# A four-layer network on one core: the front of layer 1 in two parts, and the group norm's small products tied to the scan's order

## The chip, the cores and the metric

The kernel runs on one core of one Trainium2 chip. Five engines work side by side, each through its own queue in order: TensorE (PE; its weight loads are shown as PEld), VectorE (DVE), ScalarE (ACT), GpSimd (POOL), and SyncE (SP), which here only issues DMAs. The metric is the device time in microseconds of one execution, as a median of several runs. A profile is one more execution, recorded by the hardware; its engines' busy times and waits come from that one.

## What is computed

The input is 16 images of 192 channels and 32 x 32 pixels, in fp32. Four layers follow one another, each as `x = x + layer(group_norm(x))`:

```python
x = x + L0(_gn(x))   # mLSTM block, a linear branch, 3x3 convolution, batch norm, leaky ReLU
x = x + L1(_gn(x))   # layer norm, a Mamba block, layer norm, projection
x = x + L2(_gn(x))   # depthwise 3x3 convolution, batch norm, clip to 0..6
x = x + L3(_gn(x))   # four Mamba scans of the image, depthwise branch, router
```

The group norm has 32 groups of 6 channels; each group of an image is brought to mean 0 and variance 1:

```python
def _gn(v, G=32, eps=1e-5):
    g = v.reshape(B_, G, C_ // G, H_, W_)
    m = jnp.mean(g, axis=(2, 3, 4), keepdims=True)
    s = jnp.var(g, axis=(2, 3, 4), keepdims=True)
    return ((g - m) / jnp.sqrt(s + eps)).reshape(v.shape)
```

The core of layer 1 is the Mamba recurrence over 1024 tokens, for 384 channels and 16 states n:

```python
dA = jnp.exp(dt_t[..., None] * A[None])
h = dA * h + (dt_t * x_t)[..., None] * B_t[:, None, :]
y = jnp.einsum('bdn,bn->bd', h, C_t)
```

Layer 3 has the same recurrence four times an image, in four directions.

## The kernel before

The program runs layer 0, then layers 1 and 2 together, then layer 3. A batch norm over all images separates them (layer 0 ends in one, layer 2 in one), so nothing of a later part can begin before the earlier part's last image is done.

Layers 1 and 2 (`layer12`, L1071) are one long scan of 32 units, two halves of 512 tokens for each of the 16 images. A unit has 16 steps, one for each state n, so an image has 32 steps and the part 512. One step (`scan_run`, L942) is: ACT makes three decays `da` (L987) and three scaled inputs `xbt` (L967); PE turns the inputs over into the PSUM tile `xb` (L995, L998); DVE runs three recurrences of 128 x 512 (L1011) into `h`; POOL multiplies `h` by C (L1018), which SP has loaded as `cb` two steps ahead (L969); PE adds the result into `y` (L1029), two steps later. All the scan's PE instructions are tied into one order by hand: the inner function `in_order` makes each depend on the one before, without a semaphore.

Everything else of layers 1 and 2 is side work, written as generators and handed out between the scan's instructions by the class `Side` (L210). `side.add(kind, steps, start, end)` gives a window in scan steps. At each `tick(now)` a task goes on while the units that it has yielded stay below its share of the window:

```python
share = self.totals.get(kind, self.total) * (now - start) / (end - start)
while now >= end or (task[4] < share and now >= task[5]):
```

`totals` is what the kind came to the last time (24 before that). A yielded number counts as so many units; a yielded `Wait(n)` forbids the task to go on before n steps have passed; at the end of the window all that is left is handed out at once. What is handed out is placed by a scheduler that knows the data's dependences; the engines then take their queues in order.

In an image's 32 steps the windows are, before: prep of the second half (steps 1 to 13), gating of the image before (2 to 3.5), its output product (`layer1_out`, 3.5 to 8), the gate branch of this image (`layer1_gate`, 8 to 12.5), the front of the next image (`layer1_front`, 12.5 to 20), the tail of the image before (`layer1_tail`, 13.5 to 25), gating of this image's first half (18 to 21), the convolution of the next image (`layer1_conv`, 20 to 26), layer 2 of the image before (25.5 to 34), and prep of the next image's first half (26 to 30).

`layer1_front` (L1223) loads the input x and layer 0's result, applies layer 0's batch norm and leaky ReLU in four pieces (ACT L1234, DVE L1235), adds x in four pieces (DVE L1236), stores the sum, takes the group norm, normalises (L1241), stores the result, and then goes straight on to the layer norm and the first half of the input projection (L1254 to L1259), whose result goes through DRAM to the convolution. Its tile `x1` first holds the sum and then the layer norm's result, which `layer1_gate` reads until step 12.5. `layer1_out` and `layer1_tail` share another tile of the same size, `xt`; both tiles have one buffer.

`group_norm` (L344) serves all layers. Four `bn_stats` and two `bn_aggr` on DVE give each channel's mean and variance; a product with a 96 x 96 matrix (PE, L355) averages the means over the six channels of a group; DVE copies the result out of PSUM (L357), takes the channel's difference from it (L359), squares it (L361) and adds the variance (L362); a second product (L365) averages that; ACT makes the inverse root (L367, L368). The two products have two columns each. They take a bank of the PSUM pool `mm`, which has two, for all of the side work.

Layer 0 has its own chain of PE instructions (`Chain`, L244, kept as `self.main`) and its own windows, and layer 3 calls `scan_run` with 128 units, 2048 steps.

Of the kernel before, what the change touches and what calls it, by code (L numbers as in the profile page):

```python
# [243 lines left out]
class Chain:  # L244
# [5 lines left out]
    def __call__(self, ins):  # L250
        if self.last is not None:
            why = mybir.DependencyInfo(mybir.DependencyClass.NoSync, mybir.DependencyReason.DATA)
            self.tc.add_manual_dep(ins.ins, self.last, why)
        self.last = ins.ins.name
        return ins
# [19 lines left out]
class Program:  # L275
# [68 lines left out]
    def group_norm(self, pool, psum, x):  # L344
# [4 lines left out]
        for m in range(2):  # L349
# [3 lines left out]
            yield 1  # L353
        ps = psum.tile([128, 512], F32, name="mm")
        nc.tensor.matmul(ps[:HP, :2], self.k("group", HP), mv[:, :, 0], start=True, stop=True)  # L355
        mean = pool.tile([HP, 2], F32, name="gnmean")
        nc.vector.tensor_copy(mean, ps[:HP, :2])  # L357
        d = pool.tile([HP, 2], F32, name="gnd")
        nc.vector.tensor_tensor(d, mv[:, :, 0], mean, SUB)  # L359
        q = pool.tile([HP, 2], F32, name="gnq")  # L360
        nc.vector.tensor_tensor(q, d, d, MUL)  # L361
        nc.vector.tensor_tensor(q, q, mv[:, :, 1], ADD)  # L362
        yield 1
        ps = psum.tile([128, 512], F32, name="mm")
        nc.tensor.matmul(ps[:HP, :2], self.k("group", HP), q, start=True, stop=True)  # L365
# [27 lines left out]
    def layer0(self):  # L393
        tc = self.tc
        with (
# [13 lines left out]
            self.main = Chain(tc)  # L409
            for b in range(1, self.nb):  # L410
# [19 lines left out]
            side.close()  # L430
            finish(self.layer0_spread(self.nb - 1, wp, dp))
# [510 lines left out]
    def scan_run(self, units, side, bp, psum):  # L942
# [7 lines left out]
        last = []  # L950

        def in_order(ins):

            if last:
                self.tc.add_manual_dep(
                    ins.ins, last.pop(), mybir.DependencyInfo(mybir.DependencyClass.NoSync, mybir.DependencyReason.DATA)
                )
            last.append(ins.ins.name)
# [97 lines left out]
        for i in range(len(steps) - 2, len(steps)):  # L1056
            for t in range(3):
                total(i, t)
        side.close()
# [11 lines left out]
    def layer12(self):  # L1071
        tc = self.tc
        with (
# [7 lines left out]
            self.rep = 18 * (W + 2), 6  # L1081
            self.stats = wp.tile([HP, 2, 2 * self.nb, 6], F32, name="stats")
# [18 lines left out]
            for b in range(self.nb):  # L1101
                at = 2 * NS * b
                side.add("prep", prep(units[2 * b + 1]), at + 1, at + 13)
# [3 lines left out]
                side.add("silu", self.layer1_gate(b, bp, psum), at + 8, at + 12.5)  # L1107
                if b + 1 < self.nb:
                    side.add("front", self.layer1_front(b + 1, sp, bp, psum), at + 12.5, at + 20)
                if b:  # L1110
                    side.add("tail", self.layer1_tail(b - 1, sp, bp, dp, psum), at + 13.5, at + 25)
# [600 lines left out]
```

## Time and profile before

| | us |
|---|---|
| median of three runs | 17126.98 |
| the three runs | 17106.91 to 17131.63 |
| the profiled execution's own time | 17158.12 |
| its span, first to last instruction | 17156.3 |
| first scan of layers 1 and 2 starts at | 3755.3 |
| first scan of layer 3 starts at | 7540.7 |
| last scan of layer 3 starts at | 17089.1 |

The profiled execution took 31 us longer than the median. The busy time of an engine is the union of its instructions' times; the waits of an engine are its idle stretches, each put down to the instruction that ended it. The granted clock of TensorE is 0.959 on average. Of the DMA engines 29.7% of the time is used, and the core moves 90 GB/s.

The costliest rows of the page are the scan's own: POOL's product L1018 (2560 times, 3469 ns each, 8871.5 us), ACT's decays L987 (7680 times, 714 ns), DVE's recurrence L1011 (7680 times, 1202 and 1263 ns), and PE's transposes L1029, L995 and products L998. The side work's rows are much smaller: the first small product of the group norm, L355, is two passes of 0.22 us in each of the 64 norms; the additions L1236 take 1.37 us each in the steady part, the normalisation L1241 1.80 us.

### The profile page before, as it was taken

Reading aid. Unit: us, or ns where it says so; the run is one execution under the profiler, and the core shown is the slowest. Engines: PE = TensorE matmul, PEld = TensorE weight load, DVE = VectorE, ACT = ScalarE, POOL = GpSimd, SP = SyncE. Lnnn points to the kernel's source line nnn. Section 1 sums busy time; section 2 is a strip of 40 time slices with the busy share of each in tenths; the row PEclk is TensorE's granted clock in tenths of the full one; section 3 lists DMA queues with packets and bytes.
Section 4 is the critical chain, followed back from the end, with each engine's and each line's share of the span. In section 5 each row is a group of like instructions: output and inputs, shape, how many; then the busy total and the mean of one; then the engine's idle time right before and its main releaser. Section 6 shows DMA issues by size and latency. Waiting matters only on the chain. (4 is left out here: it accounts for less than half of the span.)

```text
span 17156.3 us, 262939 instructions
## 1 busy us (share of the span) xinstructions
PE 15613.4 (91%) x99452; PEld 10979.0 (64%) x99452; DVE 13102.8 (76%) x14795; ACT 11895.7 (69%) x19766; POOL 11422.4 (67%) x5491
## 2 busy tenths in 40 slices
PE   7999999979999999979999999999999999999998
PEld 4444444446555555647777777777777777777777
DVE  4555455547777777758888888988888898888888
ACT  3333333337666766748888888888888888888888
POOL 3334443436555555638888888878888888888888
PEclk8999999989999999989999999999999999999999
DMA  1111111123334443333333323333332333333232
GB/s 52 45 47 45 47 45 46 42 76 108 117 119 121 120 120 115 100 101 107 93 96 101 109 83 101 109 91 97 100 108 84 101 109 92 96 100 107 86 98 67
DMA packets 890140, 1544.64 MB, mean 90 GB/s; under 512 B 83472, under 2 KB 314653, under 8 KB 879530
## 3 DMA queue, kind: packets, MB, share of 16 engines
q1 hardware_dynamic: 888874, 1527.81, 29.7%
q8 instruction: 788, 12.91, 0.3%
q14 instruction: 478, 3.92, 0.1%
HBM read 1284.22 MB, written 243.27 MB: 89 GB/s over the span
## 5 line engine op out<-in xcount | busy, mean ns | idle before, releaser
L1018 POOL TENSOR_TENSOR h<-h,cb 128x1536 f32<-128x1536 f32 x2560 | 8871.5, 3469 | 1439.4 <-DVE h L1011 961.0
L987 ACT ACTIVATE da<-dt,neg_a 128x512 f32<-128x512 f32 x7680 | 5267.1, 714 | 1618.4 <-DVE h L1011 1565.5
L1011 DVE TENSOR_TENSOR_SCAN h<-da,carry,xb 128x512 f32<-128x512 f32 x3840 | 4653.2, 1263 | 708.8 <-PE xb L998 672.9
L1029 PE MATMUL y<-const,h 128*128 128x128 f32 x30720 | 4710.0, 276 | 127.4 <-DVE ysum L1469 54.0
L1011 DVE TENSOR_TENSOR_SCAN h<-da,xb 128x512 f32<-128x512 f32 x3840 | 4440.8, 1202 | 388.3 <-PE xb L998 272.1
L995 PE MATMUL xb<-const,xbt 128*128 128x128 f32 x23040 | 4057.7, 281 | 379.4 <-DVE h L1011 219.9
L967 ACT ACTIVATE xbt<-ut,bt 128x384 f32<-128x384 f32 x7680 | 4174.4, 603 | 210.3 <-PE xb L995 208.7
L1029 PEld LDWEIGHTS y<-const,h 128*128 128x128 f32 x30720 | 3677.9, 143 | 343.6 <-issue 288.4
L995 PEld LDWEIGHTS xb<-const,xbt 128*128 128x128 f32 x23040 | 2750.2, 142 | 1744.0 <-issue 616.2
L998 PE MATMUL xb<-diag,ut 128*128 128x128 f32 x15360 | 3015.1, 278 | 0.0
L998 PEld LDWEIGHTS xb<-diag,ut 128*128 128x128 f32 x15360 | 2382.8, 195 | 97.9 <-issue 97.9
L831 POOL TENSOR_TENSOR hs<-h,mhm 128x384 f32<-128x384 f32 x128 | 108.5, 848 | 1570.7 <-DVE den L836 735.6
L977 POOL TENSOR_TENSOR diag<-const,bt 128x512 f32<-128x512 f32 x640 | 687.0, 1074 | 575.3 <-PE xb L998 320.8
L1017 POOL COPY carry<-h 128x3 f32<-128x3 f32 x1280 | 249.1, 195 | 1222.7 <-DVE h L1011 978.2
L705 POOL TENSOR_TENSOR e<-e,const 128x1536 f32<-128x1536 f32 x128 | 443.3, 3464 | 244.0 <-DMA e<-row 226.9
L520 PE MATMUL conv<-ya,w_conv 128*64 128x512 f32 (+1 forms) x1152 | 500.9, 646 | 99.4 <-DMA ya<-yrows 61.2
L917 PE MATMUL mm<-dbl,w_dt 45*128 45x512 f32 x960 | 536.1, 642 | 33.4 <-DVE v L1491 16.1
L711 ACT ACTIVATE e<-e 128x1536 f32<-128x1536 f32 x128 | 189.7, 1482 | 445.6 <-POOL e L706 445.6
L780 PEld LDWEIGHTS num<-v,p 128*128 128x128 f32 x3072 | 386.6, 200 | 123.6 <-issue 50.8
L921 DVE SCALAR_TENSOR_TENSOR dt<-lnsq,mm 128x512 f32<-128x512 f32 x480 | 322.2, 671 | 184.1 <-ACT lnsq L920 184.1
L1172 PE MATMUL mm<-rep,taps 128*32 128x512 f32 x3072 | 423.8, 607 | 27.9 <-DMA rep<-xr 17.8
L1172 PE MATMUL mm<-rep,t_dw 96*32 96x512 f32 x2304 | 427.0, 618 | 22.1 <-DMA rep<-xr 15.9
(273 smaller groups left out, 17446.6 us busy)
## 6 DMA issues: line engine op xcount, KB each, us to landing
cb<-row SPq DMA_DIRECT2D x2560, 256.0 KB
rep<-xr SPq DMA_DIRECT2D x384, 331.0 KB
e<-row SPq DMA_DIRECT2D x128, 768.0 KB
rep<-xin SPq DMA_DIRECT2D x384, 256.0 KB
rep<-xr SPq DMA_DIRECT2D x384, 228.8 KB
x<-x SPq DMA_DIRECT2D x48, 768.0 KB
xr<-xin SPq DMA_DIRECT2D x48, 612.5 KB
xr<-xpad SPq DMA_DIRECT2D x32, 867.0 KB
```

What stands on the lines that cost most here:

```text
L520: nc.tensor.matmul(o, self.w_c2[:k, t, c0 : c0 + o.shape[0]], src[:k, r0 : r0 + 16, dx : dx + W], start=t == 0, stop=t == 14, skip_group_c ...
L705: nc.gpsimd.tensor_tensor(k.e, k.e, self.k0("mask")[:, None, :].to_broadcast([128, NH, 128]), ADD)
L917: nc.tensor.matmul(ps, w_dt[:, t * 128 : (t + 1) * 128], dbl, start=True, stop=True)
L967: nc.scalar.activation(t[:, c], u.ut[:, c], AF.Copy, scale=u.bt[:, c, n : n + 1])
L977: nc.gpsimd.tensor_tensor(d, ident[:, None, :].to_broadcast([128, 4, 128]), u.bt[:, 3, n : n + 4][:, :, None].to_broadcast([128, 4, 128]), ...
L987: nc.scalar.activation(da[i, t], u.dt[:, t], AF.Exp, scale=u.neg_a(t, n))
L995: in_order(nc.tensor.transpose(xb[i, t][:, c * 128 : (c + 1) * 128], xbt[i][:, c, t * 128 : (t + 1) * 128], ident))
L998: in_order(nc.tensor.matmul(xb[i, t][:, 384:], u.ut[:, 3, t * 128 : (t + 1) * 128], u.diag[n // 4][:, n % 4], start=True, stop=True, skip_ ...
L1011: nc.vector.tensor_tensor_scan(hv, dv, xv, 0.0 if first else u.carry_in[:, n, t : t + 1], MUL, ADD)
L1018: nc.gpsimd.tensor_tensor(h[i], h[i], u.c.pop(n)[:, None, :].to_broadcast([128, 3, 512]), MUL)
L1029: in_order(nc.tensor.matmul(u.y[:, j], h[i][:, t, c * 128 : (c + 1) * 128], ident, is_transpose=True, start=n == 0 and j % 4 == 0, stop=n ...
L1172: self.nc.tensor.matmul(ps[32 * g : 32 * g + 32], blocks[:, g * side + r], seen, start=r == 0, stop=r == side - 1, skip_group_check=True,)
```

## The change

The change has three parts.

First, `layer1_front` ends after the normalisation and its store. The rest, the layer norm and the input projection, becomes `layer1_xin`, which reads the normalised tile `xf` that the front leaves. The front's sum now lies in the tile name `xt`, shared with the output product and the tail; `layer1_xin` makes `x1`. The windows move: `layer1_xin` takes steps 13 to 20, and the front of the image after the next takes steps 26.5 to 35, that is up to step 3 of the next image. For the second image it runs in steps 2 to 10 of the first. Each of the front's four pieces counts a whole unit instead of a half. Other windows move by up to two steps.

Second, `group_norm` yields a `Wait` of `self.pause` before each of its two products: 0 in layer 0, 0.6 from layer 1 on (layer 3 doesn't set it again). The products are also placed behind the last scan instruction handed out so far: `Chain` gets a method `behind` that adds this order without making the product a part of the chain. `scan_run` uses a `Chain` in place of its `in_order` function, and clears it at the end, as layer 0 does now.

Third, the difference is taken from the product's PSUM tile itself; the copy of the mean to SBUF comes after the square and the sum.

```diff
     def __init__(self, tc):
         self.tc, self.last = tc, None
 
-    def __call__(self, ins):
+    def behind(self, ins):
+
         if self.last is not None:
             why = mybir.DependencyInfo(mybir.DependencyClass.NoSync, mybir.DependencyReason.DATA)
             self.tc.add_manual_dep(ins.ins, self.last, why)
+        return ins
+
+    def __call__(self, ins):
+        self.behind(ins)
         self.last = ins.ins.name
         return ins
 
...
                 nc.vector.bn_stats(st[:, m, i], x[:, m, h])
             nc.vector.bn_aggr(mv[:, m], st[:, m].rearrange("p a b -> p (a b)"))
             yield 1
+        yield Wait(self.pause)
         ps = psum.tile([128, 512], F32, name="mm")
-        nc.tensor.matmul(ps[:HP, :2], self.k("group", HP), mv[:, :, 0], start=True, stop=True)
-        mean = pool.tile([HP, 2], F32, name="gnmean")
-        nc.vector.tensor_copy(mean, ps[:HP, :2])
+        self.main.behind(
+            nc.tensor.matmul(ps[:HP, :2], self.k("group", HP), mv[:, :, 0], start=True, stop=True)
+        )
         d = pool.tile([HP, 2], F32, name="gnd")
-        nc.vector.tensor_tensor(d, mv[:, :, 0], mean, SUB)
+        nc.vector.tensor_tensor(d, mv[:, :, 0], ps[:HP, :2], SUB)
         q = pool.tile([HP, 2], F32, name="gnq")
         nc.vector.tensor_tensor(q, d, d, MUL)
         nc.vector.tensor_tensor(q, q, mv[:, :, 1], ADD)
+        mean = pool.tile([HP, 2], F32, name="gnmean")
+        nc.vector.tensor_copy(mean, ps[:HP, :2])
         yield 1
+        yield Wait(self.pause)
         ps = psum.tile([128, 512], F32, name="mm")
-        nc.tensor.matmul(ps[:HP, :2], self.k("group", HP), q, start=True, stop=True)
+        self.main.behind(nc.tensor.matmul(ps[:HP, :2], self.k("group", HP), q, start=True, stop=True))
         r = pool.tile([HP, 2], F32, name="gnr")
         nc.scalar.activation(r, ps[:HP, :2], AF.Ln, bias=self.k("eps", HP))
         nc.scalar.activation(r, r, AF.Exp, scale=-0.5)
...
             n = self.nb * S // 128
             side = Side()
             self.main = Chain(tc)
+            self.pause = 0
             for b in range(1, self.nb):
                 side.add("image", self.layer0_image(b, sp, bp, psum), 8 * b - 6.2, 8 * b - 4.6)
             for i in range(1, self.nb * S // U):
...
                 for j, _ in enumerate(self.layer0_step(g, n, chunks, sp, bp, psum)):
                     side.tick(g + j / 8)
             side.close()
+            self.main.last = None
             finish(self.layer0_spread(self.nb - 1, wp, dp))
             for j in range(3):
                 finish(self.layer0_conv2(self.nb - 1, j, bp, psum))
...
         ident = self.k("ident")
         steps = [(u, n) for u in units for n in range(NS)]
         xbt, xb, da, h = {}, {}, {}, {}
-        last = []
-
-        def in_order(ins):
-
-            if last:
-                self.tc.add_manual_dep(
-                    ins.ins, last.pop(), mybir.DependencyInfo(mybir.DependencyClass.NoSync, mybir.DependencyReason.DATA)
-                )
-            last.append(ins.ins.name)
+
+        in_order = self.main = Chain(self.tc)
 
         def times_b(i):
             if i >= len(steps):
...
         for i in range(len(steps) - 2, len(steps)):
             for t in range(3):
                 total(i, t)
+        in_order.last = None
         side.close()
 
     def untranspose(self, y, t, psum):
...
         ):
             self.layer1_weights(wp, dp, psum)
             self.rep = 18 * (W + 2), 6
+            self.pause = 0.6
             self.stats = wp.tile([HP, 2, 2 * self.nb, 6], F32, name="stats")
             self.image = {b: {} for b in range(self.nb)}
             side, units = Side(), []
...
                     units.append(u)
             for b in range(self.nb):
                 at = 2 * NS * b
-                side.add("prep", prep(units[2 * b + 1]), at + 1, at + 13)
+                side.add("prep", prep(units[2 * b + 1]), at + 0.5, at + 12)
                 if b:
                     side.add("gate", self.layer1_gated(units[2 * b - 1], bp, psum), at + 2, at + 3.5)
                     side.add("out", self.layer1_out(b - 1, bp, psum), at + 3.5, at + 8)
-                side.add("silu", self.layer1_gate(b, bp, psum), at + 8, at + 12.5)
+                elif self.nb > 1:
+                    side.add("front", self.layer1_front(1, sp, bp, psum), 2, 10)
+                side.add("silu", self.layer1_gate(b, bp, psum), at + 8, at + 13)
                 if b + 1 < self.nb:
-                    side.add("front", self.layer1_front(b + 1, sp, bp, psum), at + 12.5, at + 20)
+                    side.add("xin", self.layer1_xin(b + 1, bp, psum), at + 13, at + 20)
                 if b:
-                    side.add("tail", self.layer1_tail(b - 1, sp, bp, dp, psum), at + 13.5, at + 25)
-                side.add("gate", self.layer1_gated(units[2 * b], bp, psum), at + 18, at + 21)
+                    side.add("tail", self.layer1_tail(b - 1, sp, bp, dp, psum), at + 14, at + 26)
+                side.add("gate", self.layer1_gated(units[2 * b], bp, psum), at + 18.5, at + 22)
                 if b + 1 < self.nb:
-                    side.add("conv", self.layer1_conv(b + 1, bp, psum), at + 20, at + 26)
+                    side.add("conv", self.layer1_conv(b + 1, bp, psum), at + 18, at + 24.5)
+                    side.add("prep", prep(units[2 * b + 2]), at + 24.5, at + 29.5)
                 if b:
-                    side.add("layer 2", self.layer2(b - 1, bp, psum), at + 25.5, at + 34)
-                if b + 1 < self.nb:
-                    side.add("prep", prep(units[2 * b + 2]), at + 26, at + 30)
+                    side.add("layer 2", self.layer2(b - 1, bp, psum), at + 26, at + 35)
+                if b + 2 < self.nb:
+                    side.add("front", self.layer1_front(b + 2, sp, bp, psum), at + 26.5, at + 35)
             finish(self.layer1_front(0, sp, bp, psum))
+            finish(self.layer1_xin(0, bp, psum))
             finish(self.layer1_conv(0, bp, psum))
             finish(prep(units[0]))
             self.scan_run(units, side, bp, psum)
...
     def layer1_front(self, b, sp, bp, psum):
 
         nc = self.nc
-        x = bp.tile([HP, 2, S], F32, name="x1", bufs=1)
+        x = bp.tile([HP, 2, S], F32, name="xt", bufs=1)
         nc.sync.dma_start(x, self.ins["x"][b].rearrange("(m p) t -> p m t", p=HP))
         xf = bp.tile([HP, 2, S], F32, name="xf", bufs=1)
         nc.sync.dma_start(xf, self.y0[b].rearrange("(m p) t -> p m t", p=HP))
...
                 nc.scalar.activation(v, v, AF.Identity, bias=self.bn0[:, m, 1:2], scale=self.bn0[:, m, 0:1])
                 nc.vector.scalar_tensor_tensor(v, v, 0.01, v, MUL, MAX)
                 nc.vector.tensor_tensor(x[:, m, h], x[:, m, h], v, ADD)
-                yield 0.5
+                yield 1
         nc.sync.dma_start(self.x1[b], x)
         mean, r, _ = yield from self.group_norm(sp, psum, x)
         for m in range(2):
             nc.vector.tensor_scalar(xf[:, m], x[:, m], mean[:, m : m + 1], r[:, m : m + 1], SUB, MUL)
         nc.sync.dma_start(self.xf1[b], xf)
+        self.image[b]["xf"] = xf
         yield 1
-        xn = x
+
+    def layer1_xin(self, b, bp, psum):
+
+        nc = self.nc
+        xf = self.image[b].pop("xf")
+        xn = bp.tile([HP, 2, S], F32, name="x1", bufs=1)
         for h in halves():
             yield from self.layer_norm(
                 bp, psum, [xf[:, m, h] for m in range(2)], [xn[:, m, h] for m in range(2)],
```

## The prediction

> **What bounds the kernel now.** I read the page's first two parts first, then busy time by stage, then TensorE's waits in the steady part of layers 1 and 2, then two engines' timelines around the longest of those waits.
>
> ```profile
> span 17156.3 us, 262939 instructions
> PE 15613.4 (91%) x99452; PEld 10979.0 (64%) x99452; DVE 13102.8 (76%) x14795; ACT 11895.7 (69%) x19766; POOL 11422.4 (67%) x5491
> PE   7999999979999999979999999999999999999998
> ```
>
> PE is the busiest engine everywhere, so a stage gets shorter only by the idle time of PE that is taken out of it. The same by stretches (length, then busy PE, PEld, DVE, ACT, POOL): layer 0, layers 1 and 2 in steady state, layer 3.
>
> ```profile
> 0.00:3680.00 3680.00, 3273.74 (x14468) 1704.29 (x14468) 1806.36 (x3616) 1117.38 (x1692) 1433.67 (x874) 0.91 0.18 47
> 3845.00:7080.00 3235.00, 2948.91 (x17319) 1930.90 (x17318) 2453.61 (x2674) 2253.51 (x3630) 1855.21 (x884) 0.97 0.39 117
> 7600.00:17000.00 9400.00, 8745.01 (x64140) 6944.77 (x64139) 8372.31 (x7993) 8089.19 (x13741) 7761.96 (x3550) 0.98 0.32 98
> ```
>
> The middle stretch holds 286 us in which PE does nothing, 20 us for each of some 14 images. PE's own waits there (total, times, longest) say who ends them:
>
> ```profile
> PE mm L355 <- DVE gnmv L352: 72.3, 14, 5.2
> PE mm L1065 <- ACT o L1258: 30.0, 14, 2.4
> ...
> PE xb L995 <- DVE gnd L359: 20.8, 14, 1.5
> PE mm L377 <- DVE xf L1241: 20.2, 28, 1.5
> PE mm L365 <- DVE gnq L362: 12.3, 13, 1.4
> ```
>
> Fourteen times 5.16 us: once an image, and always the first product of a group norm. One image (from 4852.5 us, 32 scan steps) cut at its steps 8, 13, 16 and 22:
>
> ```profile
> 4852.50:4904.00 51.50, 49.43 (x318) 33.94 (x317) 37.84 (x39) 37.54 (x62) 36.93 (x22) 1.00 0.21 63
> 4904.00:4934.80 30.80, 28.70 (x187) 21.94 (x186) 23.58 (x25) 19.62 (x32) 19.20 (x11) 1.00 0.14 41
> 4934.80:4960.30 25.50, 16.86 (x96) 12.67 (x95) 24.21 (x31) 17.06 (x28) 13.45 (x9) 0.87 0.40 115
> 4960.30:5014.90 54.60, 50.66 (x265) 31.63 (x263) 39.84 (x48) 38.51 (x63) 25.88 (x11) 1.00 0.45 136
> 5014.90:5080.40 65.50, 62.98 (x397) 36.65 (x397) 49.34 (x53) 47.90 (x77) 36.98 (x14) 1.00 0.62 184
> ```
>
> Only in steps 13 to 15 is DVE (24.2 of 25.5 us) the bound and PE idle (8.6 us). DVE's and PE's timelines there:
>
> ```profile
> 4939.44 5.27 DVE L1236 TENSOR_TENSOR x<-x,xf 96x512 f32<-96x512 f32 x4 [1.20 <-DMA x<-x]
> 4944.63 1.87 DVE L351 BATCH_NORM_STATS2 gnst<-x 96x6 f32<-96x512 f32 x3
> ...
> 4947.92 0.48 PE L355 MATMUL mm<-gnmv,const 96*96 96x2 f32 x2 [5.16 <-DVE gnmv L352]
> ```
>
> The front's whole residual addition and statistics go to DVE at once; the scan's next chunk waits behind them, and PE, which takes its instructions in order, has run out of work and stands at the small product.
>
> **What the Trainium skill says.** *SBUF — State Buffer*, "Who interferes with whom": a VectorE instruction with two SBUF inputs shares a read port with a GpSimd instruction that reads SBUF, and the later one blocks fully. This trace agrees: L1236 takes 0.67 us at best and 3.94 us at worst, L361 (96x2) 0.13 and 3.37 us, beside GpSimd's 3.47 us products (L1018). *Perfetto Trace Analysis*, "Optimizing Scalar/DVE Operations": a VectorE that isn't saturated but makes bubbles elsewhere is helped by smaller portions. The 5.16 us above with DVE at 76% is this case. *PSUM — Partial Sum Buffer*, "Specifications (TRN2)": eight banks of 2 KiB. Here y takes three, xb three, and all side products share the two of `mm`; the trace shows no wait put down to one.
>
> **The change, part by part.** (a) *The front is split and moved.* I laid every side task's pieces out by the pacing rule of the code (each kind's share of its window, a pause as a time before which nothing follows) and priced them by the rows of this trace, in us of PE / DVE. Scan step 3.34 (step 0's length) / 3.7 (three at 1.23). Front: four pieces of 0 / 2.05 (0.68 + 1.37), two statistics of 0 / 1.5, normalisation 0 / 3.5. Layer norm of a half 3.5 / 2.6; input projection and gate 1.76 / 0 and 1.76 / 0.75, six each; convolution 2.1 / 0.73, six; prep 9.2 / 4.2 in all, twice; output 2.64 / 0.74, four; tail's projection 3.5 / 1.46, twice; gated 0.56 / 0.74, six; layer 2's four parts 3.15 / 0.67. In each step I take the larger of PE and DVE and add up. Per image:
>
> before: steps 4-12 PE 53.8, DVE 41.1, sum of larger 53.8; 12-18: 41.7, 48.1, 56.2; 18-26: 52.1, 44.1, 53.9; 26-36: 60.1, 46.3, 62.6. Total 226.4; the trace's images 2 to 13 take 226.9 on average (from one image's first L1011 to the next one's), so the table can be trusted.
>
> after: 4-12: 52.9, 40.4, 53.3; 12-18: 41.2, 31.6, 41.5; 18-26: 55.3, 45.6, 57.5; 26-36: 58.2, 62.0, 66.7. Total 219.0.
>
> The lump comes from step 13: the old pause of one step lets a share of 24.2/7.5 = 3.2 units through together, at half a unit a piece: four additions, both statistics and a layer norm, 16.8 us of DVE against 5.4 of PE. The new front has about ten units for 8.5 steps, one piece a step. What it loses: steps 26-36, with PE at 60 of 62.6 us, receive 15.7 us of DVE, partly offset by the convolution and prep drawn 2 and 1.5 steps forward; PE and DVE are then both at about 90%. Over all sixteen images: +10.7 in the first (it gets two fronts), -5.0 to -9.6 in thirteen, -12.2 in the fifteenth: **-93 us**. The waits L355, xb after gnd and L377 (8.1 us an image) are this same loss seen from PE, so not counted again.
>
> (b) *Pauses and the hold behind the scan* (0.6 step, some 4 us, before each small product in layers 1 to 3). The pause covers the DVE operations in front of a product. L365's wait goes: 12.3 us above plus 5.5 us in layer 3. Nothing waits behind a held product that isn't its own norm. I take -10. In layer 0 the pause is zero and only the order is fixed: its L355 waits add up to 19 us, so between -19 and +30 (2 us on 15 norms); I take 0. Layer 3's L355 waits are 0.4 us: nothing to win.
>
> (c) *Difference from PSUM, mean's copy after the squares.* One SBUF read less on a 0.13 us instruction, worth nothing. But the bank is now freed after L362's successor instead of after L357: in this trace 3.6 us later in a front, 5.0 in a tail, 3.7 in layer 3, since a scan comes between any two small operations. Below: no gain possible. Above: PE stands for it all, rival D. A side product finds the other bank in most cases; I take 0.3 us on each of 45 norms, +14.
>
> (d) *Queues.* The front's two loads and two stores (768 KB each) pass on SP from steps 12-20 to 26-35, beside layer 2's `rep` loads. Its load of x now goes into `xt`, free only when the tail's normalisation is done (due step 26, load due 26.5), and the output part's load waits in the same way half a step after the front's end. SP queues `cb` loads behind such a wait; they run two steps ahead (some 14 us), which hides it. The front's own wait for x was 1.2 us each; -15 to +15 in all, I take 0. Convolution starts two steps before the projection ends, but each piece reads what was written over a step (7 us) earlier.
>
> Sum: -93 - 10 + 14 = -89. On the profiled execution's 17158 that is 17069; its own time lies 31 us above the median 17127, so the forecast for a median is **17038**.
>
> **Rivals.**
> B, *more comes out*: the other 10 us of idle an image (L1065 after o, 2.1, L1298 after xtok, 2.1, and the rest) shrink too, since gating and silu were moved by half a step. For it: PE's floor is 207 us an image. Against: those waits are between engines, not from the front. Half of it, 5 x 15 = 75 us more: 16963.
> C, *DVE jams the new place*: with PE and DVE both at 90% in steps 26-36 each waits for the other. Layer 3 runs at 93% and 89%, which speaks against; five us an image gives the gain back but for 14 us: 17113.
> D, *slower: the held bank*. If side products always want both `mm` banks while a mean is pending, PE, in order, stands for the extra hold: 15 x 3.6 + 15 x 5.0 + 15 x 3.7 = 185 us. 17127 - 103 + 185 = 17209. It decides from 2.3 us a norm (103/45). For it: layer 2 keeps a bank for three tap rows just when the new front's norm runs. Against: no bank wait in the trace, though a tail's norm already lies beside convolution.
>
> **How the numbers follow.** Forecast 0.58 (17000 to 17080), B 0.13, C 0.13, D 0.16. The measurement tells no change within 0.2%, 34 us. Forecast and B are faster, C the same, D slower: 0.71, 0.13, 0.16. The range goes down to 16970, just above B's, and up to 17150, which takes in C and leaves out most of D.
>
> **What would show it.** Right: PE's wait at L355 below 1 us an image; images of 217 to 221 us; the front's additions one by one between steps 27 and 31; layer 3 within 15 us. Wrong: idle PE before `mm` products that DVE's mean copy ends (D); DVE over 95% busy with scans late in steps 26 to 35 (C); a layer 3 or layer 0 that moves by more than 30 us, which nothing here foresees.

## The result and the profile after

| | before | after |
|---|---|---|
| median, us (4 runs each) | 17124.1 | 17022.1 |
| ratio, 95% interval | | 0.9940 (0.9928 to 0.9952) |
| profiled execution's span, us | 17156.3 | 17013.7 |
| layer 0 and weights, to the first scan | 3755.3 | 3739.5 |
| layers 1 and 2, first to last scan | 3553.2 | 3419.4 |
| layer 3, first to last scan | 9548.4 | 9556.3 |

The changed kernel is 102 us faster by the medians, where 89 us were forecast. The two profiled executions differ by 143 us, because the one before lay 34 us above the median of its four runs and the one after 7 us below. A second profile of the kernel before, below, is 42 us shorter than the first: 21 us of that are in layer 0, 18 in layers 1 and 2.

The first part of the page after:

```profile
span 17013.7 us, 263068 instructions
PE 15545.9 (91%) x99452; PEld 10952.1 (64%) x99452; DVE 13117.0 (77%) x14795; ACT 11873.8 (70%) x19766; POOL 11405.1 (67%) x5491
```

The instructions of DVE, ACT and POOL are as many as before and within 0.2% as long in sum. PE executes as many products as before; its idle time is 75 us shorter, and its busy time is 67 us shorter as well (15613.4 us before). By stretches of the changed kernel (layer 0, steady part of layers 1 and 2, layer 3; columns as before):

```profile
0.00:3665.00 3665.00, 3274.78 (x14469) 1700.76 (x14470) 1820.85 (x3616) 1117.99 (x1692) 1434.22 (x874) 0.91 0.19 47
3830.00:6990.00 3160.00, 2914.89 (x17585) 1929.07 (x17584) 2483.17 (x2697) 2261.22 (x3673) 1873.60 (x894) 0.98 0.40 121
7450.00:16860.00 9410.00, 8757.72 (x64175) 6953.32 (x64174) 8381.10 (x7997) 8093.38 (x13748) 7757.42 (x3554) 0.98 0.31 98
```

In the middle stretch PE is idle for 245 us of 3160, before 286 of 3235. The stretches hold different parts of images, so here are images 2 to 13 alone, twelve of them, from the first scan of image 2 to that of image 14: before, split_only (an experiment below) and the changed kernel.

```profile
4172.20:6894.90 2722.70, 2482.66 (x14572) 1622.40 (x14571) 2062.43 (x2256) 1897.69 (x3050) 1557.53 (x746) 0.97 0.39 117
4136.40:6808.80 2672.40, 2423.96 (x14563) 1599.37 (x14562) 2096.88 (x2256) 1875.30 (x3046) 1551.15 (x744) 0.97 0.39 119
4140.30:6754.10 2613.80, 2414.70 (x14564) 1600.05 (x14563) 2068.55 (x2255) 1876.05 (x3046) 1547.76 (x744) 0.98 0.41 122
```

An image takes 217.8 us where it took 226.9. Of these 9.1 us, 3.4 are idle time of PE (20.0 before, 16.6 after) and 5.7 are busy time (206.9 and 201.2) as the profile counts it, with modelled ends of the products. The second profile of the kernel before has 225.5 us, 19.6 of them idle. In split_only all of the gain is busy time; PE is idle for 20.7 us. More than half of the busy time went from one group, the convolution's products. Fifteen images' worth of them, before, in split_only and in the changed kernel (count, then busy time and mean ns of one):

```profile
L1273 PE MATMUL mm<-rep,t_conv 128*32 128x512 f32 x718 | 204.7, 610 | 22.8 <-DMA rep<-xin 22.4
L1285 PE MATMUL mm<-rep,t_conv 128*32 128x512 f32 x720 | 156.0, 607 | 24.5 <-DVE xt L1357 15.8 <-DMA rep<-xin 7.2 <-DVE o L1147 1.3
L1289 PE MATMUL mm<-rep,t_conv 128*32 128x512 f32 x720 | 155.3, 614 | 22.3 <-DVE xt L1361 14.3 <-DMA rep<-xin 7.0 <-DVE o L1151 0.9
```

One product is as long as before, but the products overlap one another more, and together they take 49 us less, 3.3 us an image. The convolution's window was moved by two steps in the change; with the old windows and the new group norm (norm_only, below) the same products, 720 of them, took 191.2 us. So most of the gain goes with the windows. No run moves the convolution's window alone, so what packs the products closer isn't shown.

Image 5, the one that was cut up before, at the same steps 0, 8, 13, 16, 22 and the next image's 0:

```profile
4802.50:4854.10 51.60, 48.76 (x312) 33.11 (x310) 39.29 (x44) 37.40 (x63) 36.24 (x23) 1.00 0.29 86
4854.10:4882.90 28.80, 27.05 (x174) 20.53 (x174) 22.79 (x25) 18.09 (x31) 18.22 (x10) 1.00 0.15 45
4882.90:4902.00 19.10, 17.38 (x108) 12.27 (x105) 15.24 (x19) 18.87 (x29) 12.87 (x9) 1.00 0.13 44
4902.00:4957.00 55.00, 49.39 (x247) 29.29 (x249) 38.35 (x44) 35.09 (x58) 24.74 (x10) 0.97 0.51 159
4957.00:5018.30 61.30, 57.01 (x385) 36.68 (x382) 55.88 (x62) 47.16 (x77) 36.91 (x13) 1.00 0.63 183
```

Steps 13 to 15 take 19.1 us where they took 25.5, with 1.7 us of idle PE where there were 8.6. DVE had 24.2 us of work there and has 15.2. That work now lies in the last line, steps 22 to 31, where DVE has 55.9 us instead of 49.3. This stretch didn't become longer for it: it takes 61.3 us where it took 65.5, with 57.0 us of work for PE where there were 63.0. Over the five lines together PE's idle time fell by 3 us only, from 19.3 to 16.2; what went in steps 13 to 15 came back in part in the others.

PE's longest waits in the steady part are now these; no group norm product is among them:

```profile
PE mm L394 <- ACT lnsq L393: 31.8, 42, 1.1
PE mm L1270 <- DVE xt L1361: 30.1, 15, 2.4
PE xb L999 <- ACT xbt L971: 27.3, 41, 1.3
PE mm L1314 <- ACT xtok L944: 24.5, 28, 0.9
```

DVE's timeline around the front's additions (L1246, L1236 before), one image. The first line is from the profile before: the scan that followed the additions and statistics there, which began at 4939.44.

```profile
4948.52 1.22 DVE L1011 TENSOR_TENSOR_SCAN h<-da,xb 128x512 f32<-128x512 f32 x1
...
5643.69 5.43 DVE L1246 TENSOR_TENSOR xt<-xt,xf 96x512 f32<-96x512 f32 x4
5649.04 1.27 DVE L1015 TENSOR_TENSOR_SCAN h<-da,carry,xb 128x512 f32<-128x512 f32 x1
5650.23 0.66 DVE L356 BATCH_NORM_STATS2 gnst<-xt 96x6 f32<-96x512 f32 x1
5650.82 0.66 DVE L949 TENSOR_TENSOR ut<-xtok,mm 128x512 f32<-128x512 f32 x1
5651.40 1.27 DVE L356 BATCH_NORM_STATS2 gnst<-xt 96x6 f32<-96x512 f32 x2
...
5653.19 1.25 DVE L1015 TENSOR_TENSOR_SCAN h<-da,carry,xb 128x512 f32<-128x512 f32 x1
```

The four additions still run back to back, and they still take 5.4 us. But a scan follows them at once, 5.4 us after the first of them began, and others come between the statistics. Before, the next scan came 9.1 us after it (from 4939.44 to 4948.52).

### The profile page after: what moved, and what is told of

It is laid out like the page before. It is cut to its first block, busy times and chain, and to the rows that moved or that the text cites. A ratio compares the mean times of both kernels' runs of the same rounds, so it can differ in the third digit from the quotient of the medians.

```text
span 17013.7 us, 263068 instructions
## 1 busy us (share of the span) xinstructions
PE 15545.9 (91%) x99452; PEld 10952.1 (64%) x99452; DVE 13117.0 (77%) x14795; ACT 11873.8 (70%) x19766; POOL 11405.1 (67%) x5491
## 5 line engine op out<-in xcount | busy, mean ns | idle before, releaser
L1002 PEld LDWEIGHTS xb<-diag,ut 128*128 128x128 f32 x15360 | 2374.7, 195 | 55.9 <-issue 55.9
L716 POOL TENSOR_TENSOR e<-e,const 128x1536 f32<-128x1536 f32 x128 | 443.4, 3464 | 223.8 <-DMA e<-row 207.7
L1182 PE MATMUL mm<-rep,taps 128*32 128x512 f32 x3072 | 421.9, 609 | 26.1 <-DMA rep<-xr 15.9
L580 PE MATMUL mm<-xn,w_up 96*128 96x512 f32 x768 | 400.6, 667 | 35.9 <-DVE xn L398 28.3
```

Of the source, the lines that this page charges most:

```text
L716: nc.gpsimd.tensor_tensor(k.e, k.e, self.k0("mask")[:, None, :].to_broadcast([128, NH, 128]), ADD)
L1002: in_order(nc.tensor.matmul(xb[i, t][:, 384:], u.ut[:, 3, t * 128 : (t + 1) * 128], u.diag[n // 4][:, n % 4], start=True, stop=True, skip_ ...
L1182: self.nc.tensor.matmul(ps[32 * g : 32 * g + 32], blocks[:, g * side + r], seen, start=r == 0, stop=r == side - 1, skip_group_check=True,)
```

## The experiments

Two theories stood against each other. The first, the prediction's: what costs time is where the front's DVE work lies. The second: what costs time is PE standing at the small products, so that the group norm's edits bring the gain. The columns for layers 1 and 2 and for layer 3 are from each run's profile, from the first scan to the last. Ratios are to the kernel before on the same chip. The runs came on three occasions, in which the kernel before had medians of 17125, 17151 and 17132 us, so totals are compared by ratios.

| run | median us | ratio (95%) | layers 1, 2 | layer 3 |
|---|---|---|---|---|
| before_again (one run) | 17115.7 | | 3535 | 9546 |
| split_only | 17069.3 | 0.9970 (0.9959 to 0.9982) | 3483 | 9552 |
| norm_only | 17284.6 | 1.0093 (1.0079 to 1.0107) | 3680 | 9565 |
| lump_after | 17035.6 | 0.9948 (0.9934 to 0.9961) | 3443 | 9572 |
| no_pause | 17050.9 | 0.9937 (0.9925 to 0.9950) | 3479 | 9519 |
| no_hold | 17058.3 | 0.9942 (0.9930 to 0.9955) | 3432 | 9582 |
| copy_late | 17054.2 | 0.9945 (0.9931 to 0.9959) | 3426 | 9579 |
| norm_no_pause | 17144.3 | 0.9996 (0.9988 to 1.0004) | 3582 | 9511 |
| after_again | 17028.0 | 0.9939 (0.9926 to 0.9953) | 3425 | 9562 |
| pause_12 | 16965.6 | 0.9904 (0.9891 to 0.9918) | 3416 | 9516 |
| psum_only (one run) | 17010.3 | | 3472 | 9507 |
| early_load | 16921.7 | 0.9879 (0.9866 to 0.9893) | 3374 | 9518 |

**before_again**: no edit.

> The kernel before, unchanged, for a second profile of it: how far layer 0 (3755 us to the first scan of layers 1 and 2), layers 1 and 2 (3554 us from first to last scan) and layer 3 (9550 us) move from one execution to the next. If the 16 us by which layer 0 was shorter after the change belong to the change, this profile shows 3755 again within 5 us; if they are scatter, it lies nearer to 3740. Layers 1 and 2 should come back within 10 us.

Layer 0 took 3734.5 us, layers 1 and 2 3535 us, layer 3 9546 us. The 16 us by which layer 0 was shorter after the change are scatter between executions. Layers 1 and 2 came back 18 us shorter, where at most 10 were expected; differences of less than 20 us in one profile's stretch of layers 1 and 2 are scatter. In layer 3 the two profiles differ by 2 us.

**split_only**: the changed kernel with the group norm of before.

```diff
-        yield Wait(self.pause)          # both of them
-        self.main.behind(nc.tensor.matmul(...))
+        nc.tensor.matmul(...)
-        nc.vector.tensor_tensor(d, mv[:, :, 0], ps[:HP, :2], SUB)
+        nc.vector.tensor_copy(mean, ps[:HP, :2])
+        nc.vector.tensor_tensor(d, mv[:, :, 0], mean, SUB)
```

> The changed kernel with the group norm of before: no pause, products not held behind the scan, difference from the copied mean. Theory 1 (place): what costs time is the front's DVE work lying in one lump on steps 13 to 15, so moving and spreading it brings nearly all; adding the larger of PE and DVE step by step gives 3431 us for layers 1 and 2, as for the whole change (3440): a total within 25 us of the changed kernel's 17022. Theory 2 (waits): what costs time is PE standing at the small products, which need the pause and the hold; then this brings at most 30 us, 17095 or more, and L355 or L365 still hold PE for over 2 us an image.

It brings 0.30% of the 0.60%. The total lies between the two theories. The wait at the first product is gone with the move alone, but PE now stands at the second one. PE's longest wait in its steady part:

```profile
PE mm L370 <- DVE gnq L367: 70.3, 20, 4.5
```

70 us over 14 images, as much as the first product had cost before. So the first theory isn't complete: in the new place the second product is put down too early unless something holds it back. What the 52 to 70 us by which layers 1 and 2 are shorter consist of is shown above: PE's idle time is about as before, and the convolution's products take 49 us less. This run moves the front and the other windows together, and none moves one without the other, so how much the front's new place brings by itself is not shown.

**norm_only**: the kernel before with the new group norm, front and windows as they were.

> The kernel before with the new group norm alone (pauses, hold, difference from PSUM), front and windows as before. Theory 1: the lump on DVE stays, and PE runs dry in steps 13 to 15 at another instruction; the pause moves the layer norm behind it, so 0 to 43 us less, 17081 to 17124. Theory 2: PE's waits at L355, after gnd and at L365 go (105 us of the steady part), so 17020 to 17045.

Neither: 159 us slower. The part that the first theory named is there. PE's timeline in one image, at the same point as before the change:

```profile
5647.28 0.60 PE L1033 MATMUL y<-const,h 128*128 128x128 f32 x4
5654.83 0.45 PE L999 MATMUL xb<-const,xbt 128*128 128x128 f32 x1 [6.95 <-DVE h L1015]
```

The small product has left the head of PE's queue, and PE stands even longer, at the scan's own transposes, because DVE is busy with the front's lump:

```profile
5644.37 5.47 DVE L1242 TENSOR_TENSOR x<-x,xf 96x512 f32<-96x512 f32 x4 [1.01 <-DMA x<-x]
```

That takes the wait at L355 as a cause off the list: it only marked where PE ran dry. The loss comes in steps 18, 19 and 28 (16.5, 20.1 and 18.5 us on average in images 2 to 13, before 11.1, 12.4 and 7.7), which neither theory foresaw.

**norm_no_pause**: norm_only with the pause at 0.

```diff
-            self.pause = 0.6
+            self.pause = 0
```

> The kernel before with the new group norm but no pause. With the pauses it was 159 us slower than before: images of 238 us, the lump's idle time still there at another instruction, and steps 18, 19 and 28 longer. If the two pauses are the cause (1.2 steps more in a window of 7.5, so the layer norm and the projection are crowded to its end and the convolution and prep are late), this is within 40 us of 17124. If the hold is the cause, it stays at 17230 or more.

Ratio 0.9996: as before, but two effects cancel in it. Layer 3 is 35 to 37 us shorter than before (see psum_only), and layers 1 and 2, 3582 us, are 28 to 47 us longer, on a chip where the kernel before is 26 us slower in all. Of the 127 to 145 us that norm_only lost in layers 1 and 2 the pauses make 98; the rest came with the hold and the difference from PSUM, which no run separates in the old place. In the old front everything after the norm shares one window of 7.5 steps with it. Two pauses delay the layer norm and the projection, which are then handed out at the window's end, and convolution and prep get their inputs late. That the crowding at the window's end is the mechanism fits with the three long steps and was not tried by itself.

**lump_after**: the changed kernel, the front's pieces and statistics without units, so all handed out at once.

```diff
-                yield 1                 # front's four pieces; the two statistics likewise
+                yield 0
```

> The changed kernel, but the front's four pieces and both statistics count no units, so they are handed out at once, in the new place (step 27.5), pauses and hold kept. Theory 1: the lump of 11 us of DVE is back; step by step 3513 us against 3440, so 40 to 75 us slower than the changed kernel, 17060 to 17095. Theory 2: with pauses and hold the products never stop PE, so within 15 us of 17022.

The total is within 15 us of 17022, as the second theory had it. The ratios of lump_after and of the changed kernel overlap; layers 1 and 2 are 18 to 23 us longer than in its two profiles, about half of the least that the first theory expected, and at the edge of the scatter. The run tests less than it was meant to: the four additions run back to back in the changed kernel too, so what lies differently is mainly the statistics, and from the first addition to the next scan it is 8.4 us in one image here, 5.4 there. For that, PE's new wait at the scan's transposes is 2.6 us an image (26.1 us in ten), where the lump in the old place had made it stand for 5.2. That PE has layer 2's taps and prep to work on in the new place would explain the smaller wait; it isn't shown. The step-by-step sum had priced this run 73 us above the changed kernel.

**no_pause** and **no_hold**: the changed kernel without one or the other (`self.pause = 0`; `behind` returns without adding an order).

> The changed kernel with the pause at 0 everywhere; hold and difference from PSUM kept. Without all three, PE stood 5.2 us an image at the second product and the total was 47 us above the changed kernel. If the pause is what gives DVE the time to finish before the product, that wait is back: 3 to 5 us an image at L374, 17055 to 17080. If the hold behind the scan is what counts, it stays away: within 12 us of 17022.

> The changed kernel with the two products placed freely; pauses and difference from PSUM kept. If the hold is what counts: 17055 to 17080 and the wait at L374 back. If the pause is: within 12 us of 17022. If both are needed (pauses only say when a product may be handed out, and a free product may still be placed ahead of scan products): 17040 to 17060.

By the totals neither is missed, which fits none of the three cases. The stretches say why. Without pauses layers 1 and 2 take 3479 us, as in split_only, with the wait at the second product back (43.8 us in ten images of the middle); but layer 3 takes 9519 us instead of 9556 to 9562. Without the hold both stretches, 3432 and 9582 us, are within 7 us of copy_late's on the same chip, which has it. So the pause is worth some 50 us in layers 1 and 2 (no_pause against no_hold and copy_late, on the same chip), the hold nothing that shows there beside the pauses, and in layer 3 something about the pause costs about as much.

**psum_only**: neither pause nor hold; of the group norm's edits only the difference from PSUM.

> The changed kernel with neither pause nor hold: of the group norm's edits only the difference from PSUM is left. If that edit is worth nothing, layers 1 and 2 are as with the old group norm (3483 us within 10) and layer 3 as before the change (9546 to 9552). If it is behind layer 3's gain without pauses, layer 3 takes 9511 to 9520 us.

Layer 3 takes 9507 us, layers 1 and 2 3472 us: against split_only, which differs from it in the third edit alone (3483 and 9552 us), the gain in layer 3 belongs to the difference from PSUM, the edit that the prediction priced at nothing. The group norm's and the router's small operations in layer 3 show how (line, shapes and count, then busy time and mean ns of one). Before:

```profile
L362 DVE TENSOR_TENSOR gnq<-gnq,gnmv 96x2 f32<-96x2 f32 x15 | 43.2, 2883 | 0.5
L1681 DVE TENSOR_TENSOR xm<-gnd,gnr 96x2 f32<-96x2 f32 x15 | 17.1, 1139 | 0.0
L361 DVE TENSOR_TENSOR gnq<-gnd 96x2 f32<-96x2 f32 x15 | 5.3, 352 | 0.4
```

psum_only:

```profile
L1696 DVE TENSOR_TENSOR xm<-gnd,gnr 96x2 f32<-96x2 f32 x15 | 15.6, 1039 | 0.0
L367 DVE TENSOR_TENSOR gnq<-gnq,gnmv 96x2 f32<-96x2 f32 x15 | 5.3, 352 | 0.4
L366 DVE TENSOR_TENSOR gnq<-gnd 96x2 f32<-96x2 f32 x15 | 2.9, 194 | 0.0
```

The changed kernel:

```profile
L1697 DVE TENSOR_TENSOR xm<-gnd,gnr 96x2 f32<-96x2 f32 x15 | 39.1, 2608 | 0.0
L367 DVE TENSOR_TENSOR gnq<-gnd 96x2 f32<-96x2 f32 x15 | 32.0, 2132 | 0.0
```

With the difference, and with those of them that aren't shown here, these operations take 4.6 us an image before, 1.7 in psum_only and 5.0 in the changed kernel. PE's two products behind them in the changed kernel (the last column is PE's idle time ahead of them and what ended it):

```profile
L1701 PE MATMUL mm<-p,wide 96*96 96x2 f32 x60 | 11.7, 265 | 37.0 <-DVE wide L1700 37.0
L374 PE MATMUL mm<-gnq,const 96*96 96x2 f32 x30 | 5.4, 249 | 40.3 <-DVE gnq L368 40.2
```

Before the change these two waits were 9.7 and 5.5 us, in psum_only 9.2 and 4.3. Each of the DVE operations is 96 x 2 numbers and takes 0.13 us at best. They have two SBUF inputs each, and POOL's product runs beside them. Before the change, in one image of layer 3:

```profile
10753.01 0.16 DVE L361 TENSOR_TENSOR gnq<-gnd 96x2 f32<-96x2 f32 x1
10753.05 3.46 POOL L1018 TENSOR_TENSOR h<-h,cb 128x1536 f32<-128x1536 f32 x1
10753.20 3.32 DVE L362 TENSOR_TENSOR gnq<-gnq,gnmv 96x2 f32<-96x2 f32 x1
```

POOL began 0.15 us before L362, and L362 ends when POOL does. That is what the Trainium skill states (*SBUF — State Buffer*, "Who interferes with whom"): a VectorE instruction with two SBUF inputs contends with a GpSimd one that reads SBUF, and which of them blocks is settled by the order of issue. The same place in psum_only:

```profile
10634.38 0.12 DVE L364 TENSOR_TENSOR gnd<-gnmv,mm 96x2 f32<-96x2 f32 x1
10634.43 0.14 DVE L369 COPY gnmean<-mm 96x2 f32<-96x2 f32 x1
10634.54 0.18 DVE L366 TENSOR_TENSOR gnq<-gnd 96x2 f32<-96x2 f32 x1
10634.76 0.16 DVE L367 TENSOR_TENSOR gnq<-gnq,gnmv 96x2 f32<-96x2 f32 x1
10634.79 3.48 POOL L1021 TENSOR_TENSOR h<-h,cb 128x1536 f32<-128x1536 f32 x1
```

DVE has as many operations ahead of the sum as before, but the difference doesn't wait for the copy any more and runs beside it. The sum begins 0.38 us after the first of them, before the change 0.56 us, and POOL's product 0.41 us after it in both. So the sum now comes 0.03 us ahead of POOL and misses the collision. With the pauses the square and the router's product run into POOL's again. DVE is nearly full in that part of layer 3 (68.9 of 71.3 us in steps 36 to 50 before), so 2.9 us an image less in these operations is 2.6 us less for the steps (68.7). With the pauses the steps take 72.2 us. For them the collisions aren't the whole account: in no_hold the norm's and the router's operations take 3.8 us an image, less than the 4.6 before, and layer 3 is the longest of all. PE stands 61 us at the two small products there and 77 in the changed kernel. Which of the two makes the pauses' cost is not shown.

**copy_late**: the changed kernel, the mean's copy ordered behind the squares' sum, as the text has it.

```diff
+        self.tc.add_manual_dep(copied.ins, added.ins.name, why)
```

> The changed kernel with the mean's copy forced to come after the squares' sum on DVE, as it stands in the text, so the bank of `mm` stays taken over both squares (the trace of the changed kernel shows the copy placed right after the difference instead). Rival D says that PE then waits for a bank: up to 185 us more, 17100 to 17200. The price taken in the prediction, 0.3 us a norm, gives 17036. If a second bank is always found: within 12 us of 17022.

Ratio 0.9945 against 0.9939 and 0.9940, stretches within the scatter: rival D's 185 us are ruled out, and a bank held over both squares costs nothing that shows. The prediction's own 14 us are too few to be told from nothing by the totals. In the changed kernel it isn't even held: DVE's queue has the copy right behind the difference.

**after_again** and **pause_12**: the changed kernel again, and with the pause in layers 1 and 2 alone.

```diff
             self.rep = 19 * (W + 3), 4
+            self.pause = 0
```

> The changed kernel again, beside the next three on one chip: 0.994 of the kernel before, layers 1 and 2 within 15 us of 3419 us, layer 3 at 9556 to 9582 us.

> The changed kernel with the pause at 0.6 in layers 1 and 2 and 0 in layer 3. In the runs so far layers 1 and 2 took 3419 to 3432 us with pauses and 3479 to 3483 without, but layer 3 took 9511 to 9519 us with the hold and no pause, 9556 to 9582 with pauses. If the two effects add up, this is 40 to 60 us faster than the changed kernel: a ratio of 0.9905 to 0.992, images of layer 3 at steps 36 to 50 back from 72 to 69 us. If layer 3's gain hangs on the order that layers 1 and 2 leave, or was scatter, it is within 12 us of the changed kernel.

The changed kernel came back as expected (0.9939, 3425 and 9562 us). Without pauses in layer 3, the total is 16965.6 against 17028.0 us on the same chip, 62 us less, just above the 40 to 60 expected. 46 of them are in layer 3, with steps 36 to 50 at 69.2 us; layers 1 and 2 keep what the pauses bring (3416 us).

**early_load**: pause_12, and in the tail the two pieces of x1 loaded before the layer norm.

```diff
-            self.rep = 18 * (W + 2), 6
+            self.rep = 18 * (W + 2), 5
             for h in halves():
+                o, ps = [], []
+                for m in range(2):
+                    o.append(bp.tile([128, 512], F32, name="x1t"))
+                    nc.sync.dma_start(o[m][:HP], self.x1[b, :, m, h])
                 yield from self.layer_norm(
...
-            o.append(bp.tile([128, 512], F32, name="o"))
-            nc.sync.dma_start(o[m][:HP], self.x1[b, :, m, h])
```

> As the version with pauses in layers 1 and 2 alone, and in the tail the two pieces of x1 that are added after the projection are loaded before the layer norm, into tiles of their own (one buffer of `rep` less, five for six, to make room). In the changed kernel DVE waits 4.4 us an image for that load and PE 2 to 3 us an image behind it. If that wait is what holds PE there: 25 to 45 us less than without it. If something else comes last, or the convolution misses its sixth buffer: within 12 us or slower.

44 us less than pause_12 on the same chip, at the upper end of what was expected if that wait holds PE. The wait of DVE in the changed kernel, then PE's waits behind it in pause_12:

```profile
DVE xt L1361 <- DMA o<-x1d: 62.3, 34, 5.7
```

```profile
PE mm L1270 <- DVE xt L1361: 29.2, 15, 2.4
...
PE mm L1289 <- DVE xt L1361: 14.4, 12, 2.5
```

Together 43.6 us in 14 images. In early_load neither is among PE's waits of over 7 us:

```profile
PE xb L999 <- ACT xbt L971: 37.4, 57, 1.3
PE mm L394 <- ACT lnsq L393: 30.1, 42, 1.1
PE mm L1314 <- ACT xtok L944: 26.2, 30, 0.9
```

This is the fastest version, 1.2% below the kernel before and 0.6% below the changed one.

## Why the prediction held, point by point

The time, 17022 us, lies in the range and 16 us from the forecast. That it came so near is in part luck: several sizes were wrong, one step of the mechanism was missing, and the errors cancelled.

*What bounds the kernel and where*: right about the place. Steps 13 to 15 lost most of their idle time, and norm_only shows that the wait at L355 was the mark of the lump and not its cause. Not right is that "a stage gets shorter only by the idle time of PE that is taken out of it": 5.7 of the 9.1 us an image are PE's busy time, which fell to 201 us, below the 207 us that the prediction called its floor.

*(a), -93 us for the split, the move and the spreading*: too large for what the edit does by itself. split_only's layers 1 and 2 are 52 to 70 us shorter than those of the two profiles before. The term lacks the second product's new wait, and it counts on spreading: "one piece a step" is what the pacing rule hands out, but in ten of the thirteen later images all four additions run back to back, in the others three of them; "one by one between steps 27 and 31", a sign of being right, didn't come. The Trainium skill's *Perfetto Trace Analysis*, "Optimizing Scalar/DVE Operations", which the prediction cites, speaks of breaking up instructions. The change doesn't do that (DVE has 14795 instructions before and after); it moves when they are handed out, so no run here shows what that advice is worth. For the steady images the sum came out near, 219.0 us forecast and 217.8 measured, but by another way. Its columns leave PE's own work as it was (207.7 and 207.6 us) and take 7.3 us of idle time out; measured are 3.4 us of idle and 5.7 of busy time, 3.3 of these in the convolution's products. That this came to nearly the same is luck.

*The first image, +10.7 us*: wrong in sign, 10 to 12 us less. The second image's front was priced in steps 2 to 10. In the trace of the changed kernel its additions were done before the first scan at 3739.5 us, in the prologue, where DVE has room:

```profile
L1246 DVE TENSOR_TENSOR xt<-xt,xf x8: 672/682/686, 3649.3 to 3685.7; 96x512 f32<-96x512 f32 x8
```

Eight, two images' worth. A window says when a task may be handed out, and the order in which the engines get it can be earlier.

*(b), -10 us for pauses and hold*: mis-sized in both directions. In layers 1 and 2 the pauses are worth some 50 us (3472 to 3483 us without, 3416 to 3432 with), in layer 3 they cost 46 to 63 on the same chip (9507 to 9519 without, 9556 to 9582 with, the difference from PSUM being there in both). The prediction took the waits of the old place as the price, and a stall that appears only in the new place isn't among them. "Layer 3's L355 waits are 0.4 us: nothing to win" overlooked that a pause can lose: it moves the norm's small operations beside other POOL products and up to the router's. Its sign "layer 3 within 15 us" came because this cost and the gain under (c) cancel.

*(c), difference from PSUM at nothing, the held bank at +14 us*: the first wrong, the second not borne out. DVE copies the mean right behind the difference, so the bank isn't held, and holding it (copy_late) costs nothing that shows; rival D's 185 us don't come. The difference from PSUM takes 27 to 41 us out of layer 3 (9546 to 9548 us before, 9507 to 9519 with it and without pauses). The prediction cited the port conflict and then priced the edit by the 0.13 us instruction that it shortens, instead of asking which later instruction it moves out of POOL's way.

*(d), queues at nothing*: the parts aren't nothing, and no run measures their sum. In the steady part SP waits longer for the front's transfers (76 and 68 us, before 27 and 36), and none of it shows at the head of DVE or PE. PE's wait for the convolution's loads fell from 22.4 to 7.0 us, and DVE's for x (17.0 us) is gone; DVE's wait for the tail's load of x1 grew from 42.5 to 62.3 us.

The rivals: C didn't come, though in image 5 DVE is at 91% in steps 22 to 31 and PE at 93%. B, more out of the remaining waits, came only with an edit of its own (early_load).

## What to carry to other kernels

A busy engine's work is not a fixed floor: count its busy time as well as its idle time after a change. Here the convolution's products took a quarter less of it with other windows. A wait at the head of a full engine's queue names the instruction that was unlucky, not always the cause: before moving or pausing that instruction, ask what the engine would do next, and whether the engine that it waits for has a lump there. Pacing helpers such as pauses belong to one stage's windows; a value that pays in one stage should be reset for the next, and an edit to a shared function should be timed stage by stage, because two stages can cancel. A tiny operation with two SBUF inputs is priced by the POOL operation that it may have to wait for, and where DVE is full this decides.

## What the runs showed of the hardware

A DVE operation on 96 x 2 numbers with both inputs in SBUF took 0.13 us free and up to 3.4 us beside POOL's 3.47 us product, ending with it. In layer 3 the norm's and the router's operations of this kind took 4.6 us an image before the change, 1.7 us when the difference no longer waited for the copy, and 5.0 us with the pauses. It repeats image after image (of 15 norms the sum took over 3 us in 13 before the change, in 1 in psum_only) rather than by chance. In psum_only, where that operation began 0.18 us earlier in the image shown above, the whole layer was 0.4% shorter.

The convolution's products took 0.61 us each before and after, but 718 of them kept PE busy for 205 us before and 720 for 155 us after: 2.1 of them at once on average before, 2.8 after, an estimate from count, mean and busy time.
